# A transformer block on one core: Z copied out of PSUM by ScalarE, the middle normalisation on ScalarE and GpSimd, output projections issued between the last attention products

## The chip, the core and the metric

The kernel runs on one core of one Trainium2 chip. The metric is the device time of one execution in microseconds (us); lower is better. The engines of a core run side by side, each with its own in-order instruction queue, and meet through semaphores:

- TensorE (PE in the profile; PEld is its loading of weights) multiplies matrices and writes the results to PSUM. Here PSUM has a pool of four banks for products (`ps_m`) and two score tiles (`ps_s`).
- VectorE (DVE) and ScalarE (ACT) do elementwise work and reductions and can read PSUM; GpSimd (POOL) does elementwise work on SBUF.
- SyncE (SP) issues the DMAs, in its queue's order; among them are the transposing DMAs of the softmax.

## What is computed

The reference, cut to what matters (batch 2, 1024 tokens, model width 512, 16 heads of 128, hidden width 1365, all fp32):

```python
def _layernorm(x, axis=-1, eps=1e-05):
    m = jnp.mean(x, axis=axis, keepdims=True)
    v = jnp.var(x, axis=axis, keepdims=True)
    return (x - m) / jnp.sqrt(v + eps)

def attn(x, W_Q, W_K, W_V, W_O):
    q, k, v = (einsum('bsd,hed->bhse', x, W) for W in (W_Q, W_K, W_V))
    scores = einsum('bhse,bhme->bhsm', q, k) / sqrt(128)
    scores = where(causal, -1e9, scores)
    z = einsum('bhsm,bhme->bhse', softmax(scores), v)
    return einsum('bhse,hde->bsd', z, W_O)

def ternary_quant(w):
    s = mean(abs(w))
    return clip(round(w / s), -1, 1) * s

def ffn(x, w1, w3, w2):
    w1q, w3q, w2q = map(ternary_quant, (w1, w3, w2))
    return (silu(x @ w1q.T) * (x @ w3q.T)) @ w2q.T

x1 = x + _layernorm(attn(_layernorm(x)))
out = x1 + _layernorm(ffn(_layernorm(x1)))
```

The text calls x1, the sum behind attention, the middle.

## The kernel before

**Numbers.** TensorE is fast on a short float form, `float32r`. Most operands are therefore kept as three tiles: a leading part, a low part (the rest, scaled by T12 = 4096 in some of them), and a difference of the two. A product is then a main sum of two matmuls per chunk and a third into a second bank; `combine` (lines 411 to 418), and `output_units` itself, put the two banks together. Scores and the product with V are in full fp32, which the trace shows as two matmul instructions each.

**Attention.** B = 2 batches and NP = 8 head pairs g per batch give G = 16 pairs and N = 32 heads n. The main loop (line 665) walks n, and within it i = 0 to 7, the row blocks of 128 queries; idx = 8 n + i. A row block goes through this chain:

- `scores` (505): TensorE writes s_ps; VectorE masks (515) and takes the negated maximum nm (519); ScalarE takes exp with the row sum (526); VectorE inverts the sum (531); ScalarE scales (532); GpSimd splits the fp32 words into 16-bit halves (537); a transposing DMA turns them (542).
- `join` (552): VectorE puts the turned halves together as pt (558).
- `values` (563): TensorE multiplies V with pt for two row blocks at once (572) into one PSUM bank. ScalarE writes the lead za (581), VectorE the low part zl (582), from za in SBUF and the bank in PSUM, and GpSimd the difference zd (585).

Scores are issued AHEAD = 3 row blocks before their step, `values` of a pair of row blocks three steps behind. `marks` and `behind` keep a list of each block's max, exp, half copy and turn; `with behind("max"):` makes what is traced in it issue after the latest maximum on its engine.

**Units between.** TensorE's time between the chains is filled with units that are put into `fill[i]`: `query_key_unit` and `value_unit` (projections for the next head and the next pair), `output_units(g)` (467): eight units t, one per 128 tokens, each six matmuls (473) into two banks of `ps_m` and then, on VectorE, two additions into `acc` (484 with the main bank, 487 with the difference). Units t = 0 to 3 read the z tiles of the first 512 queries, t = 4 to 7 those of the second. `block_unit(1, t)` (345) loads, normalises and transposes a block of batch 1 in head 14. `split_unit` (223) loads x1 from `mid0` in DRAM (batch 0) or takes it from `acc`, normalises it (117) and transposes it (238) for the feed-forward. `early_hidden(f)` (651) does the first three hidden tiles of the feed-forward inside the last head. `side[idx]` holds the weight statistics and the ternary weights, one small step at a time (141 to 213).

**The middle.** `middle_units(b, pool)` (244) gives sixteen units: eight `first(t)` take row statistics of the attention output (106, 107), the last of them also the reciprocal standard deviation (112, with a ScalarE table load); eight `second(t)` load x (255), normalise in place (117), add x (257), take the statistics of x1 and, for batch 0, store x1 to `mid0` (260). Batch 0's units are put into head 17, two per step; batch 1's run beside the feed-forward, two per step.

**Who sets the order.** The source order gives priorities; a scheduler traces the whole program, moves instructions within each engine's queue by readiness, and places the semaphores. `tc.issue_after(ins)` adds an order on one engine without a wait. A pool with `bufs = k` gives k buffers to each name in it; a tile that takes a buffer waits for the last reader of the one before. The pool `x` (315) of the attention part, with three buffers, holds the x tiles of `stats_load`, the weight statistics, `block_unit`, `middle_units` and `split_unit`.

**The end of attention** (735 to 739): the product for row blocks 4 and 5, the join of block 7, the product for 6 and 7, and then all eight output units of the last pair. Behind it comes the feed-forward: for each of four blocks of 512 tokens, NF = 11 steps f with a hidden unit (278) two steps ahead and `down` (765), whose loads of the ternary weights are issued at its start (749 to 828).

Of the kernel before, what the change touches and what calls it, by code (L numbers as in the profile page):

```python
# [28 lines left out]
P = 128  # L29
# [6 lines left out]
def sandwich_kernel(  # L36
# [72 lines left out]
    def reciprocal_std(mv, n, r=None):  # L109
        if r is None:  # L110
            r = small.tile([P, n], FP, name="rstd", tag=f"rstd{n}")
        nc.scalar.activation(r, mv[:, :, 1], AF.Sqrt, bias=eps)
        nc.vector.reciprocal(r, r)
        return r
# [128 lines left out]

    def middle_units(b, pool):
        mv = small.tile([P, NT, 2], FP, name="mv", tag="mv8", bufs=2)
        held = {}

        def first(t):
            row_stats(mv[:, t, :], acc[:, t, :])
            if t == NT - 1:  # L250
                held["r"] = reciprocal_std(mv, NT)

        def second(t):
            xt = pool.tile([P, D], FP, name="xt")
            nc.sync.dma_start(xt, x[b, ts(t, P), :])
            normalise(acc[:, t, :], acc[:, t, :], mv, held["r"], t)
            nc.vector.tensor_tensor(acc[:, t, :], acc[:, t, :], xt, ALU.add)
            row_stats(mv_mid[b][:, t, :], acc[:, t, :])
            if b == 0:
                nc.sync.dma_start(mid0[ts(t, P), :], acc[:, t, :])  # L260
            if t == NT - 1:
                reciprocal_std(mv_mid[b], NT, r_mid[b])

        return [lambda t=t: first(t) for t in range(NT)] + [
            lambda t=t: second(t) for t in range(NT)
        ]


# [37 lines left out]
    with ExitStack() as att:  # L306
# [5 lines left out]
        vpool = att.enter_context(tc.tile_pool(name="v", bufs=2))  # L312
        zpool = att.enter_context(tc.tile_pool(name="z", bufs=ZB))
        qpool = att.enter_context(tc.tile_pool(name="q", bufs=2))
        xpool = att.enter_context(tc.tile_pool(name="x", bufs=3))
        ps_s = att.enter_context(tc.tile_pool(name="ps_s", bufs=2, space=PSUM))


# [244 lines left out]
        def values(n, m):  # L563

            g, j = divmod(n, 2)
            qb, half = divmod(m, 2)
            if half == 0:
                zs[g, qb, j] = [zpool.tile([P, QB], FR, name="z" + f) for f in "ald"]
            ps = ps_m.tile([P, TB], FP, name="mm")
            for kt in range(2 * m + 2):  # L570
                c0 = max(0, kt - 2 * m) * P
                nc.tensor.matmul(  # L572
                    ps[:, c0:KB],
                    lhsT=proj[g, 2][:, kt, ts(j, P)],
                    rhs=pts[n, m][:, kt, c0:KB],
                    start=(kt == 0),
                    stop=(kt == 2 * m + 1),
                )

            lead, low, diff = (w[:, ts(half, KB)] for w in zs[g, qb, j])  # L580
            nc.scalar.mul(lead, ps[:, :KB], LEAD / T12)  # L581
            nc.vector.scalar_tensor_tensor(  # L582
                low, lead, -T12, ps[:, :KB], ALU.mult, ALU.add
            )
            nc.gpsimd.tensor_tensor(diff, lead, low, ALU.subtract)  # L585


        for t in range(QT):
# [76 lines left out]
        for n in range(N):  # L665
# [21 lines left out]
            if n == 2 * (NP - 1):  # L687
                units = [lambda t=t: block_unit(1, t) for t in range(NT)]
                put((4, 5, 5, 6, 6, 6, 7, 7), units)
            if n == 2 * NP + 1:  # L690
                put(sorted(2 * list(range(NT))), middle_units(0, xpool))
            splits = [lambda t=t: split_unit(0, 0, t, xpool) for t in range(QT)]
            if n == N - 2:
                put((5, 6, 7), splits)
            if n == N - 1:
                put((0,), splits[3:])
                put((2, 4, 6), [lambda f=f: early_hidden(f) for f in range(EARLY)])
            for i in range(NT):
                idx = n * NT + i
                with behind("turn", of=idx + 1):  # L700
# [9 lines left out]
                todo = fill[i]  # L710
                for u in todo[:2]:
                    u()
                if idx >= 3 and (idx - 3) % 2 == 1:
                    values((idx - 3) // NT, (idx - 3) % NT // 2)
                for u in todo[2:]:
                    u()

                with behind("max", "half", "exp", of=idx + 1):
# [7 lines left out]
                    if at < G and i in (5, 6):  # L726
                        difference_form(2 + j, at, (FRONT, BACK)[i - 5])
                look(idx + AHEAD)
                if idx > 0:
                    with behind("max"):  # L730
                        join(*order[idx - 1])
                with behind("max", "half", "turn"):
                    for u in side[idx]:
                        u()
        values(N - 1, NT // 2 - 2)
        join(N - 1, NT - 1)
        values(N - 1, NT // 2 - 1)
        for u in output_units(G - 1):
            u()

    with ExitStack() as ffn:
# [78 lines left out]
        for f in range(NF):  # L820
# [5 lines left out]
                load_t13(f, wpool.tile([P, 2, D], FR, name=("oa", "ol", "od")[k]))  # L826
            else:
                load_t13(f, tpool.tile([P, 2, D], FR, name=f"t13_{f}"))
        middle = middle_units(1, xpool)
        for n, (b, tb, f) in enumerate(steps):  # L830
            after = n // NF + 1
            if f in (2, 4, 6, 8) and after < len(steps) // NF:
                nb, ntb, _ = steps[after * NF]
                split_unit(nb, ntb, (f - 2) // 2, xpool)
            end = after == len(steps) // NF
            if end and f == NF - 4:
                ffn_hidden(*steps[n + 2])
# [9 lines left out]
                continue  # L847
            down(b, tb, f)
            with tc.issue_after(lows[-2]):
                for u in middle[:2]:  # L850
                    u()
            middle = middle[2:]
            if f == NF - 1:
                finish(b, tb)

# [42 lines left out]
```

## Time and profile before

| | us |
|---|---|
| three runs | 1569.14, 1570.14, 1571.79; median 1570.14 |
| the profiled execution | 1569.62 |
| its span, first to last instruction | 1567.6 |
| TensorE busy | 1493.4 |
| VectorE busy | 1177.0 |
| ScalarE busy | 745.4 |
| GpSimd busy | 733.3 |

The rest of the times in this document are from the profiled execution. Rows of groups give a line, an engine, an operation, what it writes and reads, how often, the busy time and the mean of one in ns, and behind the bar the idle time of the engine just before and what ended it. In the timeline a row has its start and its length in us and, in brackets, the idle time before it. Matmuls overlap: a row of 128x512 lasts about 0.39 us, and the next starts 0.23 us after it. So TensorE counts as busy a little longer than it streams. The granted clock is a share of TensorE's full speed.

TensorE's time is 0 to 56 us for the beginning, then the 32 heads to about 1310 us, some 78 us for a pair of heads, then the feed-forward. In it TensorE is busy without a gap from 1350 to 1540 us.

### The profile page before, as it was taken

The page shows a single profiled execution, that of the slowest core. Times are in us where ns is not written, and L with a number is a line of the kernel's source. Part 1 is how long each engine was busy: PE and PEld are TensorE (multiplying, and loading weights), DVE is VectorE, ACT ScalarE, POOL GpSimd, SP SyncE. Part 2 cuts the span into 40 slices and gives each one's busy share as a digit, 9 for nine tenths or more (in the row PEclk, how much of TensorE's full clock was granted, in tenths as well). Part 3 has the DMA queues.
Part 4 walks back from the last instruction along what each step waited for, and adds up shares of the span by engine and source line. Part 5 has one row for each costly group of instructions (what it writes and reads, how often), then busy time and mean ns, then how long its engine had stood idle before and what let it go on. Part 6 is the DMA issues. An engine that isn't in the chain of part 4 may idle for free. (4 is left out here: it accounts for less than half of the span.)

```text
span 1567.6 us, 20845 instructions
## 1 busy us (share of the span) xinstructions
PE 1493.4 (95%) x7078; PEld 1192.4 (76%) x7078; DVE 1177.0 (75%) x2131; ACT 745.4 (48%) x1424; POOL 733.3 (47%) x845
## 2 busy tenths in 40 slices
PE   5999999999999999999899999999989998999997
PEld 3777878787878787777677878787868876788885
DVE  5677788888887878899878888888877785754343
ACT  4555545454546455545554444444544460443333
POOL 4455455455544657665566665665554441010010
PEclk9999999999999999999999999999999998999999
DMA  2365554545454465457555555545444457210100
GB/s 82 85 132 121 115 119 108 118 107 120 108 126 107 108 119 132 111 112 168 156 115 115 115 117 112 120 115 121 108 89 88 83 113 224 70 54 0 41 28 27
DMA packets 357618, 164.94 MB, mean 105 GB/s; under 512 B 311092, under 2 KB 324404, under 8 KB 357512
## 3 DMA queue, kind: packets, MB, share of 16 engines
q1 hardware_dynamic: 357512, 163.62, 45.5%
q8 instruction: 55, 0.90, 0.2%
q14 instruction: 51, 0.42, 0.1%
HBM read 73.39 MB, written 14.68 MB: 56 GB/s over the span
## 5 line engine op out<-in xcount | busy, mean ns | idle before, releaser
L537 POOL COPY half<-p_sb 128x640 uint16<-128x640 uint16 (+7 forms) x512 | 352.2, 718 | 492.4 <-issue 288.6
L526 ACT ACTIVATE p_sb<-s_ps,nm 128x128 f32<-128x128 f32 (+7 forms) x256 | 190.0, 742 | 395.6 <-DVE nm L519 371.1
L572 PE MATMUL mm<-pt,v_sb 128*128 128x256 f32 (+1 forms) x1280 | 278.3, 365 | 26.1 <-DVE acc L484 14.5
L572 PEld LDWEIGHTS mm<-pt,v_sb 128*128 128x128 f32 x1280 | 242.4, 193 | 65.8 <-DVE acc L484 17.0
L510 PE MATMUL s_ps<-k,q 128*128 128x512 f32 (+3 forms) x768 | 289.0, 486 | 0.1
L558 DVE COPY pt<-halfT 128x256 uint16<-128x256 uint16 (+7 forms) x256 | 276.0, 1078 | 1.2 <-DMA halfT<-half 1.1
L532 ACT ACTIVATE p_sb<-p_sb,ri 128x128 f32<-128x128 f32 (+7 forms) x256 | 198.1, 774 | 93.2 <-DVE ri L531 91.5
L519 DVE TENSOR_REDUCE nm<-s_ps 128x1 f32<-128x128 f32 (+7 forms) x256 | 193.4, 755 | 6.3
L510 PEld LDWEIGHTS s_ps<-k,q 128*128 128x128 f32 x768 | 132.4, 190 | 69.1 <-issue 60.9
L453 PE MATMUL mm<-va,xb 128*128 128x256 f32 x512 | 153.1, 299 | 0.9 <-DVE acc L487 0.8
L585 POOL TENSOR_TENSOR zd<-za,zl 128x256 fp32r<-128x256 f32 x128 | 112.4, 878 | 83.9 <-DVE zl L582 60.3
L453 PE MATMUL mm<-vd,xb 128*128 128x256 f32 x512 | 145.4, 284 | 0.6 <-DVE zl L582 0.5
L453 PE MATMUL mm<-vl,xb 128*128 128x256 f32 x512 | 144.6, 282 | 0.0
L429 PE MATMUL mm<-xb,qa 128*128 128x512 f32 x256 | 120.2, 470 | 1.4 <-ACT xb L365 1.4
L429 PE MATMUL mm<-xb,ka 128*128 128x512 f32 x256 | 112.8, 441 | 2.3 <-ACT q L412 2.2
L582 DVE SCALAR_TENSOR_TENSOR zl<-za,mm 128x256 fp32r<-128x256 f32 x128 | 53.5, 418 | 79.1 <-ACT za L581 78.7
L429 PE MATMUL mm<-xb,ql 128*128 128x512 f32 x256 | 101.9, 398 | 2.5 <-DVE xb L367 2.5
L453 PEld LDWEIGHTS mm<-va,xb 128*128 128x128 f32 x512 | 97.7, 191 | 6.2 <-issue 1.9
L429 PE MATMUL mm<-xb,kl 128*128 128x512 f32 x256 | 101.9, 398 | 0.4 <-POOL kl L398 0.4
L473 PE MATMUL mm<-oa,za 128*128 128x512 f32 x256 | 95.5, 454 | 5.8 <-DVE acc L484 5.6
L453 PEld LDWEIGHTS mm<-vl,xb 128*128 128x128 f32 x512 | 97.8, 191 | 4.3 <-issue 2.4
L453 PEld LDWEIGHTS mm<-vd,xb 128*128 128x128 f32 x512 | 97.7, 191 | 1.6 <-DVE zl L582 0.7
(148 smaller groups left out, 2752.8 us busy)
## 6 DMA issues: line engine op xcount, KB each, us to landing
wqk<-wq SPq DMA_DIRECT2D x32, 256.0 KB, 3.3
wqk<-wk SPq DMA_DIRECT2D x32, 256.0 KB, 3.2
wvo<-wv SPq DMA_DIRECT2D x16, 512.0 KB, 3.8
wvo<-wo SPq DMA_DIRECT2D x16, 512.0 KB, 3.8
xt<-x SPq DMA_DIRECT2D x32, 256.0 KB, 3.1
raw<-w SPq DMA_DIRECT2D x30, 256.0 KB, 3.2
tern<-raw SPq DMA_DIRECT2D x30, 256.0 KB, 2.7
xt<-w SPq DMA_DIRECT2D x24, 227.5 KB, 3.1
```

The lines of the kernel that those rows point to most:

```text
L429: nc.tensor.matmul(main, lhsT=forms[f][0][:, c, :], rhs=forms[f][1][:, c, :], start=(c == 0 and f == 0), stop=(c == NC - 1 and f == 1),)
L453: nc.tensor.matmul((main, main, diff)[f][:, ts(t, 2 * P)], lhsT=forms[f][0][:, c, token], rhs=forms[f][1][:, c, :], start=(t == 0 and c == ...
L473: nc.tensor.matmul((main, main, diff)[f], lhsT=zs[g, t // QT, j][f][:, ts(t % QT, P)], rhs=weights[3, g][f][:, 2 * j : 2 * j + 2, :], star ...
L510: nc.tensor.matmul(s_ps[:, ds(k0, kl)], lhsT=proj[n, 0, i // QT][:, ts(i % QT, P)], rhs=proj[n, 1, k0 // TB][:, :kl], start=True, stop=True,)
L519: top = nc.vector.tensor_reduce(nm, s_ps[:, :L], axis=AX.X, op=ALU.max, negate=True)
L526: e = nc.scalar.activation(p_sb[:, :L], s_ps[:, :L], AF.Exp, bias=nm, accum_out=rs)
L532: nc.scalar.mul(p_sb[:, :L], p_sb[:, :L], ri)
L537: copy = nc.gpsimd.tensor_copy(half[:, ds(k * L, L)], words[:, :L, k])
L558: nc.vector.tensor_copy(words[:, 0 : i + 1, :, ts(il, P)], turned[:, 0 : 2 * (i + 1), :].rearrange("p (k t) q -> p t k q", k=2),)
L572: nc.tensor.matmul(ps[:, c0:KB], lhsT=proj[g, 2][:, kt, ts(j, P)], rhs=pts[n, m][:, kt, c0:KB], start=(kt == 0), stop=(kt == 2 * m + 1),)
L582: nc.vector.scalar_tensor_tensor(low, lead, -T12, ps[:, :KB], ALU.mult, ALU.add)
L585: nc.gpsimd.tensor_tensor(diff, lead, low, ALU.subtract)
```

## The change

Three things are changed, and what they need.

- `values` no longer makes zl from PSUM. ScalarE copies the bank to a new SBUF tile zf (two buffers of 128x256 fp32), and `values` returns a function `rest` that makes zl from za and zf on VectorE and zd on GpSimd. The main loop calls it behind the maximum of the scores issued last, ahead of the join.
- `middle_units` gives four lists. `second` loads x and normalises in place on ScalarE (Identity with scale and bias; the bias is a new tile, shift), `added` adds x on GpSimd, `third` takes the statistics and stores. Batch 0's are put into heads 16, 17 and the first steps of 18; batch 1's run three per step, and the splits of the next feed-forward block stand at f = 4, 6, 7, 8 in place of 2, 4, 6, 8. The x pool has two buffers in place of three.
- At the end of attention two output units of the last pair are issued ahead of the product for row blocks 4 and 5, two between it and the last product, four behind that. The three early hidden units move from steps 2, 4, 6 of the last head to 3, 5, 7.

```diff
--- before.py
+++ after.py
@@ -243,26 +243,38 @@
 
     def middle_units(b, pool):
         mv = small.tile([P, NT, 2], FP, name="mv", tag="mv8", bufs=2)
+        shift = small.tile([P, NT], FP, name="shift_mv", bufs=1)
         held = {}
 
         def first(t):
             row_stats(mv[:, t, :], acc[:, t, :])
             if t == NT - 1:
-                held["r"] = reciprocal_std(mv, NT)
+                held["r"] = r = reciprocal_std(mv, NT)
+                nc.vector.scalar_tensor_tensor(
+                    shift, mv[:, :, 0], -1.0, r, ALU.mult, ALU.mult
+                )
 
         def second(t):
-            xt = pool.tile([P, D], FP, name="xt")
+            held[t] = xt = pool.tile([P, D], FP, name="xt")
             nc.sync.dma_start(xt, x[b, ts(t, P), :])
-            normalise(acc[:, t, :], acc[:, t, :], mv, held["r"], t)
-            nc.vector.tensor_tensor(acc[:, t, :], acc[:, t, :], xt, ALU.add)
+            nc.scalar.activation(
+                acc[:, t, :], acc[:, t, :], AF.Identity,
+                scale=held["r"][:, t : t + 1], bias=shift[:, t : t + 1],
+            )
+
+        def added(t):
+            nc.gpsimd.tensor_tensor(acc[:, t, :], acc[:, t, :], held[t], ALU.add)
+
+        def third(t):
             row_stats(mv_mid[b][:, t, :], acc[:, t, :])
             if b == 0:
                 nc.sync.dma_start(mid0[ts(t, P), :], acc[:, t, :])
             if t == NT - 1:
                 reciprocal_std(mv_mid[b], NT, r_mid[b])
 
-        return [lambda t=t: first(t) for t in range(NT)] + [
-            lambda t=t: second(t) for t in range(NT)
+        return [
+            [lambda do=do, t=t: do(t) for t in range(NT)]
+            for do in (first, second, added, third)
         ]
 
 
@@ -312,7 +324,7 @@
         vpool = att.enter_context(tc.tile_pool(name="v", bufs=2))
         zpool = att.enter_context(tc.tile_pool(name="z", bufs=ZB))
         qpool = att.enter_context(tc.tile_pool(name="q", bufs=2))
-        xpool = att.enter_context(tc.tile_pool(name="x", bufs=3))
+        xpool = att.enter_context(tc.tile_pool(name="x", bufs=2))
         ps_s = att.enter_context(tc.tile_pool(name="ps_s", bufs=2, space=PSUM))
 
 
@@ -579,10 +591,16 @@
 
             lead, low, diff = (w[:, ts(half, KB)] for w in zs[g, qb, j])
             nc.scalar.mul(lead, ps[:, :KB], LEAD / T12)
-            nc.vector.scalar_tensor_tensor(
-                low, lead, -T12, ps[:, :KB], ALU.mult, ALU.add
-            )
-            nc.gpsimd.tensor_tensor(diff, lead, low, ALU.subtract)
+            copy = zpool.tile([P, KB], FP, name="zf", bufs=2)
+            nc.scalar.copy(copy, ps[:, :KB])
+
+            def rest():
+                nc.vector.scalar_tensor_tensor(
+                    low, lead, -T12, copy, ALU.mult, ALU.add
+                )
+                nc.gpsimd.tensor_tensor(diff, lead, low, ALU.subtract)
+
+            return rest
 
 
         for t in range(QT):
@@ -687,14 +705,22 @@
             if n == 2 * (NP - 1):
                 units = [lambda t=t: block_unit(1, t) for t in range(NT)]
                 put((4, 5, 5, 6, 6, 6, 7, 7), units)
+            if n == 2 * NP:
+                first, second, added, third = middle_units(0, xpool)
+                put((2, 3, 4, 6, 7), first)
             if n == 2 * NP + 1:
-                put(sorted(2 * list(range(NT))), middle_units(0, xpool))
+                put((0, 0, 0), first[5:])
+                put((1, 1, 2, 3, 4, 5, 6, 7), second)
+                put((2, 2, 3, 4, 5, 6, 7), added)
+                put((4, 4, 5, 6, 7, 7), third)
+            if n == 2 * NP + 2:
+                put((0, 1, 1), added[7:] + third[6:])
             splits = [lambda t=t: split_unit(0, 0, t, xpool) for t in range(QT)]
             if n == N - 2:
                 put((5, 6, 7), splits)
             if n == N - 1:
                 put((0,), splits[3:])
-                put((2, 4, 6), [lambda f=f: early_hidden(f) for f in range(EARLY)])
+                put((3, 5, 7), [lambda f=f: early_hidden(f) for f in range(EARLY)])
             for i in range(NT):
                 idx = n * NT + i
                 with behind("turn", of=idx + 1):
@@ -710,8 +736,9 @@
                 todo = fill[i]
                 for u in todo[:2]:
                     u()
+                rest = None
                 if idx >= 3 and (idx - 3) % 2 == 1:
-                    values((idx - 3) // NT, (idx - 3) % NT // 2)
+                    rest = values((idx - 3) // NT, (idx - 3) % NT // 2)
                 for u in todo[2:]:
                     u()
 
@@ -726,16 +753,24 @@
                     if at < G and i in (5, 6):
                         difference_form(2 + j, at, (FRONT, BACK)[i - 5])
                 look(idx + AHEAD)
+                if rest:
+                    with behind("max"):
+                        rest()
                 if idx > 0:
                     with behind("max"):
                         join(*order[idx - 1])
                 with behind("max", "half", "turn"):
                     for u in side[idx]:
                         u()
-        values(N - 1, NT // 2 - 2)
+        outs = output_units(G - 1)
+        for u in outs[:2]:
+            u()
+        values(N - 1, NT // 2 - 2)()
+        for u in outs[2:QT]:
+            u()
         join(N - 1, NT - 1)
-        values(N - 1, NT // 2 - 1)
-        for u in output_units(G - 1):
+        values(N - 1, NT // 2 - 1)()
+        for u in outs[QT:]:
             u()
 
     with ExitStack() as ffn:
@@ -826,12 +861,16 @@
                 load_t13(f, wpool.tile([P, 2, D], FR, name=("oa", "ol", "od")[k]))
             else:
                 load_t13(f, tpool.tile([P, 2, D], FR, name=f"t13_{f}"))
-        middle = middle_units(1, xpool)
+        first, second, added, third = middle_units(1, xpool)
+        middle = first + second[:1]
+        for t in range(NT):
+            middle += second[t + 1 : t + 2] + added[t : t + 1] + third[max(t - 1, 0) : t]
+        middle += third[NT - 1 :]
         for n, (b, tb, f) in enumerate(steps):
             after = n // NF + 1
-            if f in (2, 4, 6, 8) and after < len(steps) // NF:
+            if f in (4, 6, 7, 8) and after < len(steps) // NF:
                 nb, ntb, _ = steps[after * NF]
-                split_unit(nb, ntb, (f - 2) // 2, xpool)
+                split_unit(nb, ntb, (4, 6, 7, 8).index(f), xpool)
             end = after == len(steps) // NF
             if end and f == NF - 4:
                 ffn_hidden(*steps[n + 2])
@@ -847,9 +886,9 @@
                 continue
             down(b, tb, f)
             with tc.issue_after(lows[-2]):
-                for u in middle[:2]:
+                for u in middle[:3]:
                     u()
-            middle = middle[2:]
+            middle = middle[3:]
             if f == NF - 1:
                 finish(b, tb)
 
```

## The prediction

> **What bounds the kernel now.** I read the busy shares and the slices first, then what TensorE waited for, then the busy time head by head, then the timeline where TensorE stood still.
>
> ```profile
> PE 1493.4 (95%) x7078; PEld 1192.4 (76%) x7078; DVE 1177.0 (75%) x2131; ACT 745.4 (48%) x1424; POOL 733.3 (47%) x845
> ...
> PE   5999999999999999999899999999989998999997
> ...
> PEclk9999999999999999999999999999999998999999
> ```
>
> TensorE works 95% of the span. Besides the two ends three slices (39.2 us each) show an 8: those from 745, from 1137 and from 1293 us, the last with a lower clock. A change that removes no matmul can gain only from TensorE's pauses: 1567.6 - 1493.4 = 74 us in all, of which 9.6 lie before the first matmul and 10.9 in the last window of 28 us.
>
> The waits of all engines say what ended the pauses (total us, times, longest us):
>
> ```profile
> DVE zl L582 <- ACT za L581: 78.7, 92, 6.9
> ...
> PE mm L572 <- DVE acc L484: 14.5, 10, 4.0
> ...
> PE mm L572 <- DVE pt L558: 7.2, 3, 3.4
> ...
> PE mm L473 <- DVE acc L484: 5.6, 4, 2.0
> ...
> PE trx L238 <- DVE xt L117: 3.1, 1, 3.1
> ```
>
> The change has three targets here: VectorE's 78.7 us of standing before zl, the products that wait for pt, and (next view) the heads of the middle units. Windows of heads 17 to 20, cut at the maxima of VectorE; columns: busy time and count of PE, PEld, DVE, ACT, POOL, then clock, DMA share, GB/s:
>
> ```profile
> 717.00:761.00 44.00, 39.92 (x190) 30.18 (x189) 42.50 (x84) 22.44 (x43) 24.37 (x24) 1.00 0.71 187
> 761.00:803.00 42.00, 37.52 (x169) 28.68 (x169) 32.00 (x57) 23.52 (x46) 24.45 (x29) 1.00 0.49 115
> 803.00:840.00 37.00, 37.00 (x194) 30.28 (x193) 29.91 (x53) 19.21 (x39) 22.51 (x26) 1.00 0.59 120
> 840.00:881.00 41.00, 39.36 (x182) 31.07 (x181) 34.28 (x63) 18.29 (x37) 25.09 (x28) 1.00 0.49 112
> ```
>
> Heads 19 and 20 are an ordinary odd and even one: 37 and 41 us, TensorE idle for 0 and 1.64. Head 17 takes 44, with VectorE at 97% and TensorE idle for 4.08; head 18 takes 42, with 4.48 idle. That is 8 us over the ordinary pair, and TensorE's idle is 6.9 over. The end of attention, in order of time:
>
> ```profile
> 1294.42 4.08 PE L572 MATMUL mm<-pt,v_sb 128*128 128x256 f32 x12 [3.05 <-DVE pt L558]
> ...
> 1300.45 1.30 DVE L558 COPY pt<-halfT 128x2048 uint16<-128x2048 uint16 x1 [1.08 <-DMA halfT<-half]
> ```
>
> The next product waits again, 3.40 us, until 1301.90. All of output_units(G - 1), which needs neither, begins at 1307.96. The two waits also cost clock:
>
> ```profile
> 1302.00:1305.00 3.00, 3.00 (x7) 2.39 (x8) 0.00 (x0) 0.00 (x0) 0.00 (x0) 0.50 0.00 0
> 1305.00:1308.00 3.00, 3.00 (x11) 2.41 (x9) 0.00 (x0) 0.00 (x0) 0.00 (x0) 0.56 0.00 0
> ```
>
> Over 1290 to 1320 the granted clock is 0.83, so 30 x 0.17 = 5.1 us are lost besides the 6.45 us of waiting.
>
> **The change, part by part.**
>
> *Output units between the last products.* A unit is 6 matmuls that start 0.228 us apart, 1.37 us; a pair 2.74. If pt came at the old times, the pair in front of the first product would leave 0.3 us of its 3.05 us wait. That product is 12 matmuls at 0.216 = 2.6 us, to 1297.0; the second pair runs to 1299.7; the last product (16 x 0.216 = 3.5 us) starts at 1301.9 and ends at 1305.4 at full clock; the four units left end at 1310.9. Before, eight units from 1307.96 end at 1318.9. That is 8.0 us. Two things take some back. The early hidden units move one step later, and in the built program's order ScalarE now loads a table, runs exp on 896 columns, loads, runs silu, scales, loads, and only then runs exp on 1024: one table load of 1.28 us and a silu of 0.69 more than before stand ahead of the last exp, some 2 us. And the second unit's diff bank is the one that the last early hidden unit frees at VectorE's L297, which the new order puts behind the join of row block 6; TensorE stands until then, at worst 3 to 5 us. I take half of the worst: 8.0 - 3.5 = 4.5 us gained. Ends: 0 (both in full, with a new clock drop) and 11.6 (all waiting and all half clock gone).
>
> The rows around the waits fit a rule of the Trainium skill, TensorE: Matmul & The Clock Gate, Part 1 (the HAM clock gate): an idle window of about 3.4 us drops the array to half clock. The trace agrees where it can: the 4.01 us wait at 1153 was followed by a clock of 0.57, the 2.23 us wait at 784 by none. By that rule shortened waits give back all 5.1 us, and this term would be nearer 8 than 4.5.
>
> *Middle units of batch 0.* For each of 8 blocks a normalise (L117 on acc, 0.593) and an add (L257, 0.730) leave VectorE: 8 x 1.323 = 10.6 us. ScalarE gets 8 Identity activations, 8 x 0.804 (the row L354 on acc) = 6.4 us; GpSimd 8 adds, 8 x 1.448 (L795) = 11.6. Two bn_stats pairs a block stay (0.678 + 0.173 each), and one shift of 0.44 (L340's row) is new. Spreading over two heads moves little: in the built order the first statistics stand among the same maxima of head 16 as before, since the scheduler had already pulled them there, and loads, activations, adds and second statistics all stand in head 17. So head 17 is the place: VectorE's 42.5 us there become 32.3 of 44, near head 18's share and under head 20's, and the 6.9 us of extra idle can go, at most the 8 us of extra time. The price: the adds fill the first half of head 17, where GpSimd has some 12 us of its own work in 22 (24.37 of 44) and gets 11.6 more, so it falls behind by a few us; an add waits for its load and its activation with the half copies of the next row block behind it; a load waits for the add two blocks earlier on SP's queue, with halfT transposes behind it; the store to mid0 now waits for GpSimd's add instead of VectorE's. What hides this is that scores run three row blocks ahead, some 15 us. I take 4.5 gained; ends 8 gained, 4 lost (about three adds on the softmax path, cover gone).
>
> *x pool from 3 buffers to 2.* Head 14's block_unit(1, t) loads (L353) wait for the transposes of the block before last. Three units stand in one step there; a bare load is 3.1 us and its activation 0.81. TensorE already idles 3.92 us of the 46 us of that head (window 589 to 635). I take 1 lost; ends 0 and 4. The mean and stats loads have one load out at a time, so two buffers do.
>
> *Z copied by ScalarE.* ScalarE gets 128 copies of 128x256 out of PSUM at L581's 0.376 us: 48 us on an engine with 52% free, which waits 371.1 us for the maximum before exp. zl keeps its count; it leaves the place where VectorE stood 78.7 us for za. I do not count that as gain: in front of the repeated wait it is not what is late.
>
> ```profile
> 997.96 1.75 DVE L208 SCALAR_TENSOR_TENSOR raw<-raw,scales,tmp 128x512 f32<-128x512 f32 x1 [0.46 <-POOL tmp L204]
> ...
> 1000.37 3.51 PE L572 MATMUL mm<-pt,v_sb 128*128 128x256 f32 x16 [1.87 <-DVE acc L484]
> ```
>
> The product waits for a bank that L484 frees, and L484 stands behind L558 and the 1.75 us L208, which waits for GpSimd; zl is in front of all of them in the old order and in the new. If the removed waits did count, up to 14.5 + 5.6 = 20.1 us would go; the lower end is a loss, since zl now reads two SBUF tiles. Rows for that:
>
> ```profile
> L582 DVE SCALAR_TENSOR_TENSOR zl<-za,mm 128x256 fp32r<-128x256 f32 x128 | 53.5, 418 | 79.1 <-ACT za L581 78.7
> ...
> L404 DVE SCALAR_TENSOR_TENSOR qd<-ql,qa 128x512 fp32r<-128x512 f32 x32 | 29.8, 931 | 2.0 <-POOL ql L398 1.8
> ...
> L404 DVE SCALAR_TENSOR_TENSOR kd<-kl,ka 128x512 fp32r<-128x512 f32 x32 | 23.3, 729 | 2.0 <-POOL kl L398 2.0
> ```
>
> L582 with a PSUM operand took 393 to 424 ns at all times. L404 has one shape and two SBUF operands in its four rows, and means of 713, 729, 761 and 931 ns: the same instruction is longer where GpSimd works beside it (longest 1.76 us). L208, of that kind too, goes from 0.75 to 1.77 us on its full tiles. The four means average 784 ns, 0.12 us above the shortest 0.66. At 0.12 a zl that is 15 us of VectorE, which idles 18% there; on TensorE's path only the zl ahead of each of 16 head pairs' bank wait, 2 us, against about 1 us for banks freed by ScalarE earlier. Net 1 us lost. Ends: 16 lost (1.0 in each pair) and 20 gained.
>
> The Trainium skill's GPSIMD Engine Reference (Specifications) says that VectorE instructions with two SBUF inputs contend with GpSimd. That speaks against this part, and L404 and L208 bear it out; L582's own row could not show it.
>
> *Feed-forward.* At 1330 the transposes wait 3.13 us for the mid load, issued behind thirty weight loads. The first split moves from f = 2 to f = 4, two down/hidden pairs later, but its xt buffer is now freed by GpSimd's first add, behind eight row statistics and a sqrt. I take 1.5 gained; ends 3.1 gained, 2 lost. The rest costs nothing: from 1350 to 1540 TensorE is busy in every window, VectorE about half, GpSimd at most 6 us in 40. Were that cover gone, batch 1's adds would cost 11.6 us.
>
> Sum: -4.5 - 4.5 + 1 + 1 - 1.5 = -8.5 us. The profiled execution took 1569.62 us with a span of 1567.6, so 2.0 us lie around it: 1559.1 + 2.0 = 1561.1. The median of the runs shown is 1570.14, 0.5 above the profiled one. I say **1561**.
>
> **Rivals.** *Contention decides (slower).* Each zl meets a GpSimd instruction that starts in it and VectorE's releases of acc slide: 16 pairs x 1.0 = 16 us, and the middle's GpSimd adds meet them too, so that gain falls to 0: 1569.6 + 16 + 1 - 4.5 - 1.5 = 1580.6; without the 16 this is 1564.6, so it decides (over 1573.3) from 8.7 / 16 = 0.55 us a pair. For: L404 qd, L208. Against: VectorE has 18% free, and GpSimd is idle more than half the time.
>
> *The ends do not fill.* The bank behind L297 and the table loads eat the whole end term and the split still waits: 1569.6 - 4.5 + 2 = 1567. For: the order of the built program. Against: 5.5 us of matmuls are free to run there.
>
> *VectorE's wait did matter.* zl out of the way shortens half of the 20.1 us: 1561 - 10 = 1551. For: 92 waits. Against: the timeline at 998.
>
> **How the numbers follow.** Forecast, 1556 to 1565: 0.50. Ends not filled, 1565 to 1573: 0.22. Contention, over 1573: 0.16. VectorE's wait, under 1556: 0.12. A difference of 0.2% (3 us) is what can be told from none, so faster is under 1567.0: 0.50 + 0.12 + about 0.09 of the second case = 0.71; slower, over 1573.3: 0.16; within: 0.13. Leaving out a tenth at each end, the range is 1550 to 1575; the forecast's own is 1556 to 1565.
>
> **What would show it.** Right: at the end of attention the waits for pt below 1.5 us and a clock over 0.9; heads 17 and 18 together near 82 us and TensorE's idle there under 5; the wait for acc L484 still 13 to 17 us; zl's mean 0.45 to 0.6 us with a tail over 0.8. Wrong: a TensorE wait named for acc or raw (L297) between the last products, GpSimd's half copies waiting for acc in head 17, zl's mean over 0.8, or the acc waits nearly gone.

## The result and the profile after

The changed kernel takes 1546.4 us (median of four runs, 1546.2 to 1546.95), the kernel before 1570.1 beside it: a ratio of 0.985, 95% interval 0.983 to 0.987. That is 23.7 us faster, where 9 were forecast. The profiled execution has a span of 1544.5 us, 23.1 less.

The page, busy shares and slices of the kernel after:

```profile
PE 1486.2 (96%) x7078; PEld 1187.2 (77%) x7078; DVE 1171.5 (76%) x2101; ACT 791.5 (51%) x1568; POOL 788.5 (51%) x861
...
PE   5999999999999998998999999999999999999997
...
PEclk9999999999999999999999999999999999999998
```

The three slices that showed an 8 before show a 9 now. Two others show an 8: the one from 579 us, in head 14, where batch 1's blocks are loaded, and the one from 695 us, before and at the start of head 17. The waits of all engines (total us, times, longest us):

```profile
PE mm L584 <- DVE acc L496: 6.7, 8, 1.0
...
PE mm L485 <- DVE acc L496: 4.6, 5, 1.3
...
DVE zl L598 <- ACT zf L595: 3.6, 9, 1.2
...
PE trx L238 <- DVE xt L117: 2.3, 1, 2.3
...
PE mm L584 <- DVE pt L570: 1.1, 1, 1.1
```

VectorE's standing before zl fell from 78.7 to 3.6 us, as meant. TensorE's wait for acc, which the prediction left as it was, fell from 14.5 + 5.6 = 20.1 to 6.7 + 4.6 = 11.3 us. Windows of heads 17 and 18 (busy time and count of PE, PEld, DVE, ACT, POOL, then clock, DMA share, GB/s):

```profile
709.00:753.00 44.00, 38.97 (x188) 30.80 (x188) 37.20 (x70) 31.77 (x58) 33.47 (x32) 0.96 0.80 195
753.00:793.00 40.00, 39.47 (x181) 30.97 (x180) 31.77 (x55) 22.96 (x49) 26.78 (x29) 1.00 0.50 112
```

Head 17 still takes 44 us and leaves TensorE idle for 5.0, though VectorE works 37.2 of them instead of 42.5; the gain of 2 us is in head 18. The end of attention, TensorE's timeline and a window over it:

```profile
1273.23 1.78 PE L584 MATMUL mm<-pt,v_sb 128*128 128x256 f32 x8 [1.10 <-DVE pt L570]
...
1281.18 0.73 PE L485 MATMUL mm<-oa,za 128*128 128x512 f32 x2 [1.13 <-ACT raw L306]
...
1283.38 2.65 PE L584 MATMUL mm<-pt,v_sb 128*128 128x256 f32 x12
...
1288.63 3.41 PE L584 MATMUL mm<-pt,v_sb 128*128 128x256 f32 x16
```

```profile
1273.00:1303.00 30.00, 28.30 (x125) 22.87 (x126) 24.68 (x42) 9.68 (x16) 8.61 (x8) 1.00 0.49 133
```

The last two products, which waited 3.05 and 3.40 us, now wait for nothing, and the clock over such 30 us is 1.00 instead of 0.83.

**Where the time came from.** Both kernels issue the same 768 score matmuls. Taking the end of each in the two traces, the changed kernel is ahead by:

| at | ahead, us |
|---|---|
| first score matmul (before any head) | 2.2 |
| head 14 | 8.0 |
| head 17 | 8.2 |
| head 20 | 10.1 |
| head 28 | 11.1 |
| head 30 | 15.9 |
| feed-forward, from 1390 us of before | 22.8 to 23.3 |

So some 6 us come in heads 0 to 13 and 4.9 in head 28 to 29, where of the edits only Z's, with the x pool, is at work; 1.9 in heads 17 to 19, and 6.9 at the end of attention and the first split. The first stretch needs a control, since nothing was edited there.

### The profile page after: what moved, and what is told of

It reads as the page before. It is cut to its first block, busy times and chain, and to the rows that moved or that the text cites. A ratio compares the mean times of both kernels' runs of the same rounds, so it can differ in the third digit from the quotient of the medians.

```text
span 1544.5 us, 21108 instructions
## 1 busy us (share of the span) xinstructions
PE 1486.2 (96%) x7078; PEld 1187.2 (77%) x7078; DVE 1171.5 (76%) x2101; ACT 791.5 (51%) x1568; POOL 788.5 (51%) x861
## 4 chain that ended last, share of the span: by engine, by line
PE 43%; DVE 5%; issue 3%; POOL 2%; ACT 1%; DMA 1%; SPq 0%; DVEq 0%; POOLq 0%; ACTq 0%
PE mm L298 10%; PE mm L584 7%; PE s_ps L522 5%; PE mm L441 5%; PE mm L465 5%; PE yp L806 5%; PE mm L485 4%; PE mm L446 3%; DVE pt L570 1%; POOL half L549 1%; POOL tmp L204 1%; DVE nm L531 1%; DVE acc L496 0%; PE trx L238 0%; DMA xt<-mid 0%
## 5 line engine op out<-in xcount | busy, mean ns | idle before, releaser
L549 POOL COPY half<-p_sb 128x640 uint16<-128x640 uint16 (+7 forms) x512 | 348.6, 710 | 443.0 <-issue 300.1
L570 DVE COPY pt<-halfT 128x256 uint16<-128x256 uint16 (+7 forms) x256 | 286.8, 1121 | 0.5 <-DMA halfT<-half 0.5
L584 PE MATMUL mm<-pt,v_sb 128*128 128x256 f32 (+1 forms) x1280 | 271.4, 359 | 9.2 <-DVE acc L496 6.7
L584 PEld LDWEIGHTS mm<-pt,v_sb 128*128 128x128 f32 x1280 | 238.9, 190 | 52.0 <-DVE acc L496 14.2
L601 POOL TENSOR_TENSOR zd<-za,zl 128x256 fp32r<-128x256 f32 x128 | 148.4, 1159 | 73.4 <-DVE zl L598 73.4
L527 DVE TENSOR_TENSOR s_ps<-s_ps,causal 128x128 f32<-128x128 f32 x256 | 75.0, 293 | 94.0 <-PE s_ps L522 93.2
```

Source lines behind the costliest of these rows:

```text
L549: copy = nc.gpsimd.tensor_copy(half[:, ds(k * L, L)], words[:, :L, k])
L570: nc.vector.tensor_copy(words[:, 0 : i + 1, :, ts(il, P)], turned[:, 0 : 2 * (i + 1), :].rearrange("p (k t) q -> p t k q", k=2),)
L584: nc.tensor.matmul(ps[:, c0:KB], lhsT=proj[g, 2][:, kt, ts(j, P)], rhs=pts[n, m][:, kt, c0:KB], start=(kt == 0), stop=(kt == 2 * m + 1),)
```

## The experiments

All ratios are against runs of the kernel before on the same chip. "Before" in a diff is the kernel before.

**The kernel before once more** (no edit).

> The kernel before, unchanged, profiled once more. Lining up equal matmuls of the two profiles, 2.2 us of the 23.1 us lie before 31 us, where nothing was edited, and 4.9 us at the single wait at 1153 us. If both belong to the execution and not to the program, this profile shows a first score matmul at 28.8 instead of 31.0 us and a wait for acc L484 near 1153 of 0.6 to 2.3 us like the other pairs, and a span of 1562 to 1566. If they belong to the program: 31.0, about 4 us, and a span of 1566 to 1569.

It took 1571.2 us with a span of 1569.3. Its first score matmul came 1.1 us earlier than in the first profile, and in the other profiles that follow 0.5 to 2.7: the start differs by that much between executions. The wait at 1153 stayed, 4.0 us long, with a clock of 0.64 over the 4 us behind it. So up to 2 us of the 23.1 are the execution's, and the 4.9 us in head 28 to 29 are the program's.

**The three parts, each alone in the kernel before.** Z alone (copy, and `rest()` behind the maximum; x pool at 2):

> Only the Z part (copy by ScalarE, zl and zd behind the later maximum), with the x pool at 2, which it needs for room. The theory after the result (VectorE's wait for za did matter for the banks): 9 to 14 us faster, 1556 to 1561, the wait of the products for acc L484 down from 14.5 to about 7 us, the wait at 1153 down to about 1. The prediction's theory (the copy is neutral and the small pool costs a little): 1570 to 1573, acc wait 13 to 17 us. Contention: 1580 or more, zl's mean over 0.8 us.

The output units between the last products, with `put((3, 5, 7), ...)` for the early hidden units:

> Only the output units between the last products, with the early hidden units one step later. By the lined-up matmuls (15.95 us ahead at 1255, 22.8 at the end): 5.5 to 7.5 us faster, 1562.5 to 1564.5, all of it after 1280 us. The prediction's theory: 4.5 us faster, 1565.6, with a wait for raw L297 between the last products. The rival that the ends do not fill: 1569 to 1571.

The middle units in four stages:

> Only the middle units in four stages (Identity on ScalarE, add on GpSimd, over two heads), the x pool left at 3. By the lined-up matmuls (8.15 us ahead at 698, 10.08 at 817): 1 to 3 us faster, 1567 to 1569, heads 17 and 18 together 83 to 85 us. The prediction's theory: 4.5 us faster, 1565.6, near 82 us. Rival: in the changed kernel the small x pool takes back what the middle units give, then here 5 us or more faster.

Z alone: 1561.0 us, ratio 0.9935 (0.991 to 0.996): the prediction's term of +1 falls here, by its sign. The middle alone: 1568.6, ratio 0.9988 (0.9977 to 1.000), some 2 us. The output units alone: 1571.9, ratio 1.0015 (1.0001 to 1.003): no gain at all, against all that was expected of them, mine after the result included. The reason stands in that run's profile, TensorE first and then SyncE's queue:

```profile
1302.77 2.65 PE L572 MATMUL mm<-pt,v_sb 128*128 128x256 f32 x12 [0.20 <-DVE raw L297]
...
1308.03 3.40 PE L572 MATMUL mm<-pt,v_sb 128*128 128x256 f32 x16
...
1335.38 1.08 PE L238 MATMUL trx<-ident,xt 128*128 128x128 f32 x4 [7.58 <-DVE xt L117]
```

```profile
1311.50 1.74 SPq L757 DMA_DIRECT2D t<-tern  x4
```

The last two products lost their waits, as intended. The feed-forward's loads of weights begin at 1311.50, right behind the last product's end (1308.03 + 3.40); in the kernel before at 1308.28, behind 1308.20. The first load of x1 from DRAM (xt<-mid) stands behind all of them and is issued 17.0 us later (1328.5; before: 1325.8, 17.5 later). That interval begins with the last product and does not shrink when TensorE has less left to do in it: four units instead of eight. So the transposes wait 7.58 us instead of 3.13, and what was won in front of them is waited out: against the kernel before, this profile is 1.8 us behind at head 30, 2.2 ahead at the last matmul in front of the transposes, and 2.3 behind when they start. Not all of the waiting for pt went, either: an earlier product, for row blocks 2 and 3, now waits 2.92 us for it, at 1292.

**The output units and the split's later place.** Both together, then the split alone:

```diff
-            if f in (2, 4, 6, 8) and after < len(steps) // NF:
+            if f in (4, 6, 7, 8) and after < len(steps) // NF:
```

> The output units between the last products and the later places of the feed-forward's first split, nothing else. My theory after the output units alone (no gain, while the transposes' wait for the first mid load grew from 3.3 to 7.9 us): the load is issued some 17 us after the last product with V, whatever TensorE does meanwhile, so time won at the end of attention is waited out there, unless the split comes later. Then 1565 to 1568 here, 4 to 6 us under the units alone, and the transposes wait under 3 us. Rival: the units gain nothing in themselves, and the split moves by itself: 1570 to 1572.

> Only the later places of the feed-forward's splits (4, 6, 7, 8 in place of 2, 4, 6, 8). My theory: it can give back no more than the 3.3 us that the transposes wait in the kernel before: 1567 to 1569. The prediction: 1.5 us faster, 1568.6. Rival (the split is worth the same as beside the units): 4 to 6 us faster, 1565 to 1567.

Together 1561.1 us, ratio 0.9946 (0.993 to 0.996), 8.8 us by the medians and 4 more than expected; the split alone 1566.0, ratio 0.998 (0.997 to 0.999), 3.9. Neither profile has a wait of trx for xt any more. So -8.8 together, where the two alone give +1.3 and -3.9: the split's later place is what lets the output units count.

**The two halves of the Z part.** Place without copy:

```diff
-            copy = zpool.tile([P, KB], FP, name="zf", bufs=2)
-            nc.scalar.copy(copy, ps[:, :KB])
...
-                    low, lead, -T12, copy, ALU.mult, ALU.add
+                    low, lead, -T12, ps[:, :KB], ALU.mult, ALU.add
```

> The Z part without its copy: the low part behind the later maximum, but read from PSUM as before, x pool at 2. If the place in the queues is what matters (GpSimd's difference no longer meets L208 but the copy into pt): as the whole Z part, 1558 to 1563, L208 in front of the acc wait at 1.15 us instead of 1.7, and 1.1 instead of 4.7 at 1153. If the early release of the bank matters, it keeps the bank longer: 1568 to 1576, and waits for zl or za at the products.

Copy without place (`values(...)()` where it stood, nothing behind the maximum):

> The Z part's copy without the place: zl is made at once, from the copy in SBUF, x pool at 2. If the place matters: 1569 to 1573, L208 at 1.7 and 4.7 us as before. If the copy's early release of the bank matters: 1558 to 1563. Contention on zl by itself would show as a zl mean over 0.6 us and 1573 to 1580.

Place without copy: 1559.6, ratio 0.9936 (0.992 to 0.995), the same as the whole part. Copy without place: 1588.4, ratio 1.0125 (1.011 to 1.014), above everything that was expected. The zl group in the two, the place first:

```profile
L584 DVE SCALAR_TENSOR_TENSOR zl<-za,mm 128x256 fp32r<-128x256 f32 x128 | 52.5, 410 | 9.0 <-ACT za L581 8.8
```

```profile
L586 DVE SCALAR_TENSOR_TENSOR zl<-za,zf 128x256 fp32r<-128x256 f32 x128 | 76.1, 594 | 72.7 <-ACT zf L583 72.0
```

The copy gives zl a second SBUF operand and makes it 0.18 us longer at the old place (128 x 0.18 = 23 us of VectorE), and VectorE still stands 72 us before it. TensorE pays 18 us for the copy and the smaller x pool together, spread over the heads with no single wait that holds them. The pool alone gave 1.004 (below), so the copy's own share is nearer 13 us; how it divides was not settled. All of the gain is in the place.

**What is left, and a kernel without the copy.** Without the copy there is room for three x buffers again:

> The changed kernel without the copy of Z (low part behind the maximum, read from PSUM) and so with room for three x buffers again. If the copy gives nothing, 1544 to 1546.5, zl's mean 0.41 us instead of 0.54, and head 14 without the extra waits for xt L366. Rival (beside the output units the copy's early release of the bank does count): 1548 to 1552.

1544.0 us, ratio 0.982 (0.981 to 0.984): 2.4 us under the changed kernel by the medians and 3.9 by the ratios. Then with two buffers of their own (`xm`) for batch 1's x in the feed-forward:

> The kernel before this one, with two buffers of their own for batch 1's x in the feed-forward, so that the first mid load no longer waits for GpSimd's first add. If that wait is what is left of the split's stall, the transposes' wait of 2.5 us goes and it is 2 to 2.5 us faster than the run without it. Rival (the load is late because of the weight loads anyway): within 0.7 us of it.

1542.2 (1542.0 to 1544.5, against 1543.5 to 1544.25), 1.8 us less by the medians, and TensorE's wait for the first split's xt is gone: GpSimd's first add had held that buffer. The changed kernel with the old middle units:

> The changed kernel with the old middle units, all else as changed. By the middle units alone (2.0 us faster than before): 1547.5 to 1549.5. By the prediction's term of 4.5 us: 1551. Rival (the new batch 1 order costs 2.5 us at the first split, and that eats the gain): 1545 to 1547.

1550.3, ratio 0.9863 against 0.9848 of the changed kernel, 2.4 us, with intervals that overlap: the middle is worth about the same beside the other parts as alone. The x pool alone:

> The x pool at 2 buffers in the kernel before, nothing else. The prediction: 1 us slower, 1571 (0 to 4). If the pool is what eats part of the Z part's gain: 1572 to 1574. If it is free: 1569 to 1570.5.

1578.1 us, ratio 1.004 (1.0025 to 1.0055), but between 1573.6 and 1581.4 from run to run: dearer than every expectation, with a size that I can't give closer. What it costs beside the place is compared below.

**What the place acts on.** At a pair's bank wait a product stands for the bank that L484 frees. In VectorE's queue side work stands in front of L484: from 500 us on L208 (a step of the ternary weights), before that L148 (a sum of the weight statistics). The wait at 1153 in the kernel before, VectorE, GpSimd and TensorE in order of time:

```profile
1150.50 1.55 DVE L558 COPY pt<-halfT 128x2048 uint16<-128x2048 uint16 x1
...
1150.82 2.34 POOL L398 TENSOR_TENSOR ql<-wqk,qa 128x512 fp32r<-128x512 f32 x1
...
1152.02 4.70 DVE L208 SCALAR_TENSOR_TENSOR raw<-raw,scales,tmp 85x512 f32<-85x512 f32 x1
...
1153.11 0.72 POOL L585 TENSOR_TENSOR zd<-za,zl 128x256 fp32r<-128x256 f32 x1
1153.78 1.17 POOL L537 COPY half<-p_sb 128x512 uint16<-128x512 uint16 x2
1154.91 1.26 POOL L398 TENSOR_TENSOR kl<-wqk,ka 128x512 fp32r<-128x512 f32 x1
...
1156.64 1.27 DVE L484 SCALAR_TENSOR_TENSOR acc<-mm,acc 128x512 f32<-128x512 f32 x2
...
1157.37 1.19 PE L572 MATMUL mm<-pt,v_sb 128*128 128x256 f32 x2 [4.01 <-DVE acc L484]
```

and the same place in the changed kernel:

```profile
1139.73 1.29 POOL L410 TENSOR_TENSOR ql<-wqk,qa 128x512 fp32r<-128x512 f32 x1
1139.78 2.45 DVE L570 COPY pt<-halfT 128x2048 uint16<-128x2048 uint16 x1
...
1140.99 1.78 POOL L601 TENSOR_TENSOR zd<-za,zl 128x256 fp32r<-128x256 f32 x1
...
1142.16 1.16 DVE L208 SCALAR_TENSOR_TENSOR raw<-raw,scales,tmp 85x512 f32<-85x512 f32 x1
...
1143.98 1.35 PE L584 MATMUL mm<-pt,v_sb 128*128 128x256 f32 x5 [0.81 <-DVE acc L496]
```

Before, the copy into pt starts 0.3 us ahead of ql: the copy takes 1.55 us and ql 2.34, and L208, which comes while GpSimd is at work, lasts until the last of GpSimd's instructions in a row (ql, zd, two half copies, kl) has ended at 1156.17, and 0.55 us more. In the changed kernel zl (0.41) stands between the maximum and the copy, the copy starts 0.05 us behind ql: now the copy takes 2.45 and ql 1.29, GpSimd is through earlier, and L208 takes 1.16. So it is with the other pairs, on a smaller scale. At the eight bank waits from 500 us on, L208 took 1.69 to 1.75 us six times before, where it met ql, once 1.14 and once the 4.70; in the changed kernel it meets the end of zd at all eight and takes 1.14 to 1.16. That is 16.2 us against 9.2, 7.0 less, and the eight waits for acc fell by 7.1, from 13.8 to 6.7 us. Pair by pair the two don't match (the third wait fell by 0.7 us with L208 at 1.14 in both). Two runs, the next one and the one behind it but one, leave Z alone and move the side work instead. First the ternary weight steps, one row block later:

```diff
-        at += (1 - at) % 4 + 4
+        at += (2 - at) % 4 + 4
```

> The kernel before with the ternary weight steps one row block later; Z untouched. L208 then stands no longer ahead of L484 where a product waits for its bank. If that meeting (L208 held by GpSimd, 1.69 to 1.75 us, once 4.70) makes the bank waits from 515 us on: these fall from 1.2 to 2.1 us to about 1, the one at 1153 from 4.6 to about 1, and it is 6 to 10 us faster, 1561 to 1565, with the waits before 500 us unchanged. If VectorE's order with zl at the front makes them: no more than 2 us faster, waits as before.

1557.0 us, ratio 0.991 (0.990 to 0.9925), 13.3 us faster with one digit. The waits up to 500 us stayed, 5.3 us instead of 5.6; behind that those of the products nearly went (waits of the window 500 to 1240, the kernel before and this one):

```profile
PE mm L572 <- DVE acc L484: 13.8, 8, 4.0
```

```profile
PE mm L572 <- DVE acc L484: 0.9, 1, 0.9
```

In the same window others came: 1.9 us for acc at L473 and 1.8 more than before behind L487. The gain is more than expected, by 3 us. Then the place by itself, with the x pool at 3:

> The low part of Z behind the maximum, read from PSUM, x pool left at 3, nothing else. If the smaller x pool cost the earlier run without the copy 2 to 4 us in head 14: 1556 to 1558. If the pool costs nothing beside the place: 1559 to 1560.5.

1557.4 us, ratio 0.9914 (0.990 to 0.993). With the pool at 2 it had been 0.9936: by the ratios the pool costs 3.5 us here, by the medians 2.2, and the two intervals overlap. Lined up, the two runs have won the same between their first score matmul and head 30 (13.4 and 13.6 us), so the cost does not lie in head 14, as was expected, but behind head 30. By lined-up matmuls the place gains 8.6 us in heads 1 to 11, where no L208 runs, and 4.9 at 1153. In these heads L148 is in front of L484, and it waits for its load and not for GpSimd. At the bank wait of 232 us, the kernel before and the changed kernel, where TensorE waits 0.98 us and not at all:

```profile
232.22 0.63 DVE L148 TENSOR_REDUCE part<-xt 128x1 f32<-128x455 f32 x1 [1.76 <-DMA xt<-w]
```

```profile
226.15 0.63 DVE L148 TENSOR_REDUCE part<-xt 128x1 f32<-128x455 f32 x1 [0.74 <-DMA xt<-w]
```

Over the whole run L148 waits 13.2 us for its loads in the kernel before, 8.3 with the place alone and 9.5 in the changed kernel; TensorE's 5.6 us of early waits for acc fall to 1.3 and 3.8. Why the place shortens L148's wait was not followed. So for the early part the weight sums (L148) and the statistics behind them, one row block later (`at = 1` for `at = 0`), Z as in the kernel before:

> The kernel before with the weight sums (loads of w, L148) and the row statistics behind them one row block later; Z untouched. If L148 ahead of L484, waiting for its load, makes the early bank waits: those at 232, 310, 388 and 467 us (0.9 to 2.3 us) go, 4 to 7 us faster, 1563 to 1566. If VectorE's standing for za makes them: the waits stay and it is within 2 us of before. The waits from 515 us on stay in both.

1558.8 us, ratio 0.993 (0.991 to 0.994), 11.2 us, where 4 to 7 were expected. The waits at 232, 310, 388 and 467 us are gone, and L148 waits 3.3 us in all; the waits from 503 on are as they were, 4.0 us at the last included. That is the other half: those waits go without Z being touched.

**The early hidden units.**

> The changed kernel with the early hidden units at steps 2, 4, 6 as before. The prediction: table loads and a silu ahead of the last exp cost some 2 us at 3, 5, 7, so 1544 to 1545 here. Rival (at 2, 4, 6 they collide with the last scores as in the Z part alone, where pt came 2 to 4 us later): 1547.5 to 1550.

1548.7 us, ratio 0.9859: the later steps gain some 2 us (2.3 by the medians, 1.7 by the ratios, whose intervals overlap); the prediction had charged 2 for them.

**Joined.** No copy, x pool 3, own x buffers, and the weight steps one row block later; then the sums too:

> The fastest so far (no copy, x pool 3, own x buffers for batch 1) with the ternary weight steps one row block later. If L208 still costs at the pairs' bank waits (1.05 us each, eight of them): 1536 to 1540. If the place of Z has taken all there was: 1541.5 to 1543.

> The joined kernel with the weight sums one row block later too. In it only one early bank wait is left (1.6 us at 381 us): at most 2 us faster, 1537.5 to 1539; if the place has taken all of that, or the statistics now meet another wait: 1539 to 1541.

1539.6 us, ratio 0.980 (0.978 to 0.982), and 1536.9, ratio 0.979 (0.977 to 0.980): 9.5 us under the changed kernel. Moving the steps gives 2.6 us on top of the place, the sums 2.8 more: place and shifted side work for the most part remove the same waits.

## Why the prediction was right in direction and wrong in size

**The step that failed** is the Z part: "I do not count that as gain: in front of the repeated wait it is not what is late", with "zl is in front of all of them in the old order and in the new", and +1 us. The run with Z alone shows -9.6, the place alone -12.9. zl was indeed not late itself. But its move from before the mask and the maximum to right between the maximum and the copy into pt shifts when VectorE's two-operand and copy instructions meet GpSimd's. The prediction saw L208 in that queue at 1.75 us and knew why it is long, and then took its length as given, though the order that made it was being edited; and it does not name the longest one, 4.70 us, which stood in front of the 4.01 us wait that it does name. What the runs showed in its place: from 500 us on L208 at the bank waits is shorter by 7.0 us in all, and TensorE's waits for acc there by 7.1; in the early heads it is L148's wait for its load that is shorter, for a reason that stays open. The term that VectorE's waits for acc stay at 20.1 us failed with it: 8.8 us went, and with the 4.0 us one its lower clock.

The rival that VectorE's wait did matter had the sign and put the gain at half of the 20.1 us, but 1546.4 lies under its 1551 too, and its mechanism is not what the runs show: those with moved side work remove the same waits while VectorE stands before zl nearly as long as before (71.5 us in the first of them).

**Contention** was right as a mechanism, and its price of 16 us is near what the copy costs at the old place (some 13, with the smaller pool 18); that it is near is in part luck, since it was put on the 16 pairs' bank waits alone and the cost is spread over the heads. At the new place zl's mean is 0.54 us, inside the forecast 0.45 to 0.6, and no cost shows: with the copy 0.9935, without it 0.9936.

**The ends and the split** were forecast at 4.5 + 1.5 = 6.0 and measured at 8.8. Of the steps behind the 4.5, in the changed kernel the waits for pt and the clock came as in the ideal sum; the bank of the last early hidden unit cost 1.1 us (the wait named for ScalarE's raw, L306) instead of 3 to 5; and the 2 us charged for the later steps of the early hidden units were of the wrong sign (the run with the old steps). What the sum lacked is that the two terms hang together: without the split the units are worth nothing.

**The middle** was forecast at 4.5 and is worth 2. VectorE was relieved of 5.3 us in head 17 (42.5 to 37.2), half of the 10.2 computed: beside GpSimd, which now works 33.5 of the 44 us, its instructions with two operands grew there (od from 0.72 to 1.46 us, kd from 0.66 to 1.20, L208 from 0.98 to 1.43, zl, which now reads two SBUF tiles, from 0.41 to 0.72). TensorE idles 5.0 us there as against 4.1, at a clock of 0.96; heads 17 and 18 take 84 us, not 82. What holds head 17 now was not settled.

**The x pool** was forecast at 1, all of it in head 14. Beside the place the runs give 2.2 to 3.5, with intervals that overlap and behind head 30; alone some 6, with runs 8 us apart.

The parts alone, in one line: -9.6 (Z with pool and copy) - 8.8 - 2.0 = -20.4 of -23.7. Z alone leaves the last products waiting 0.76, 2.35 and 4.19 us for pt, and its lead falls from 13.5 us at head 30 to 11.5 at the end; with the output units between, that loss does not arise. That would be 2 of the missing 3.3 us; the rest was not pinned down, and the intervals of the three ratios, 2 to 3 us to either side, are wide enough to hold all of it.

## What to carry to other kernels

A wait that repeats at the same step of a loop is worth moving side work away from before anything is made cheaper: two one-digit shifts of the weights' side work gave 13 and 11 us, as much as the best form of the rearrangement of Z (12.9). When an edit changes an engine's order, the length of an instruction that meets another engine there must be worked out anew, not read from the old row. And time won in front of a chain of loads that starts at a fixed event is lost again at the end of that chain, unless its first consumer is moved too.

## What the runs showed of the hardware

**VectorE waits for GpSimd's whole instruction, and can miss its turn.** L208 on its full tiles takes 0.75 us where it meets no GpSimd instruction with two operands. Otherwise it ends some 0.55 us behind the end of the one that it met (ql, zd or xb): 1.14, 1.22, 1.69 and 1.75 us, for ends at 0.59, 0.67, 1.14 and 1.20 us after its start. The Trainium skill, SBUF — State Buffer (Who interferes with whom), says that the one who issues first holds the shared ports for the whole instruction, and that issue order decides. The swap of pt's copy and ql above (1.55 and 2.34 us against 2.45 and 1.29) agrees. But the 4.70 us L208 stood through the ends of ql, zd and two half copies and ran only behind kl, and it did so in all nine profiles in which it stood at that place with zl at its old one (4.69 to 4.73 us), and in none of the others, where no L208 took over 1.78 us. Why it missed its turn is open, the more so as half copies beside it left it at 0.75 us in the run with the weight steps moved.

**A lower clock after a 2 us wait, in some profiles.** The same wait near 390 us, 1.9 to 2.0 us long, left the clock at 1.00 in four profiles (the kernel before twice, and the two runs with the split's later place), and was followed by 4 us windows at 0.58, 0.71 and 0.65 in three (the output units alone, the middle alone, the weight steps later), though their edits too stand behind that point. So a single execution's clock behind such a wait says little (nor does the 2.23 us wait that left the clock alone, which the prediction took as a sign), and an edit elsewhere can seem to cost some 1.7 us there, worked out as 4 us times the clock that is missing in that window and the one beside it.
